# A four-layer adaLN block on one core: where the inputs are turned, where the keys come from, and four reordered slots

## The chip, the core and the metric

The kernel runs on 1 core of a Trainium2 chip. A core has five engines, each with an instruction stream of its own that is worked off in order: TensorE (PE in the profile; PEld is its weight load), VectorE (DVE), ScalarE (ACT), GpSimd (POOL) and SyncE (SP), which here only issues DMAs. ACT and POOL issue DMAs too. Engines wait for one another by semaphores. The metric is the device time of one execution in microseconds (us). Before the change three timed runs gave 6840.84, 6856.30 and 6861.61 us, with the median 6856.3.

## What is computed

The reference is a stack of four layers on x of 32 sequences x 256 positions x 128 features, all in float32. Each layer has an attention half and a feed-forward half, each wrapped in adaptive layer norm:

```python
mod = (_silu(Ln_c) @ Ln_wmod).reshape(32, 6, 1, 128)      # shift, scale, gate, twice
sa, ca, ga, sb, cb, gb = (mod[:, i] for i in range(6))
g* = (2 * (g* >= 0) - 1) * jnp.maximum(jnp.abs(g*), 0.25)
x = x + ga * attn(_layernorm(x) * (1 + ca) + sa)
x = x + gb * ffn(_layernorm(x) * (1 + cb) + sb)
```

The change touches three places of it. The beginning reads x and makes the modulations of the four layers. Layer 0's attention half is a selective scan (h = exp(delta A) h + delta u B, y = C h, over 256 positions, 16 states for each feature, two branches that share the scan), with delta and u from a softplus. Layer 1's attention half has a windowed softmax attention and five sets of causal linear attention: the plain keys and values, and four levels of keys and values averaged over blocks of 2, 4, 8 and 16, each set with features phi(k) = elu(k) + 1, a running sum over the sequence in chunks of 128, and a division by the norm. The other halves (two mixtures of experts, two more attentions, a grouped MLP, an fp4 MLP) are not touched.

## The kernel before

x is cut into 16 tiles of 512 positions (two sequences), and kept turned (features on the partitions) in on-chip memory for the whole run; `self.mods` keeps all modulations. `run` calls `begin`, then one body per half.

`begin` loads the c and wmod of all four layers in one DMA on ACT's queue, makes the four layers' modulations (six matmuls each, then copies on ACT and six operations on DVE for each of two halves), and turns the 16 tiles: one load each, by turns on SP's and ACT's queue with three buffers, four transposes on PE, and a copy by turns on DVE and ACT. Its pools close before those of the next body open.

`scan_layer` and `hale` are each an agenda: work is put under a slot number, and slots are emitted in order. PE's instructions keep exactly this order (`mm` and `tr` ask for it), in the scan ACT's too. Instructions of DVE and POOL and DMAs do not: a scheduler (the tile framework's) places them in their engine's stream by its own estimate of when they are ready, so a slot number alone does not tell where they stand.

In `scan_layer`, tile b's scan occupies slots 16b to 16b+15, and its preparation (two layer norms, projections, softplus for u and delta, B and C spread) slots 16b-40 to 16b; so 40 slots lead in before the first scan. A pass p (two slots, 8 passes a tile) is: 16 matmuls into `dB`, four DVE scans from `dB` and four `decay` tiles that ACT made a pass earlier, and, for the pass before, two sets of eight transposes into `hT` (one buffer), two ACT copies to `hsT`, and two sets of matmuls (`scan_weigh`) that add into `y`. `dB`, `hT`, `y` and `tp` have one PSUM buffer each. The softplus is split: `soft_start` makes |v+b| on ACT and max(v+b, 0) on DVE from a PSUM tile `tp`, `soft_end` makes ln(1+exp(-|v+b|)) on ACT and adds on POOL. A tile ends with `scan_end` in slot 16b+19: four transposes, an addition on DVE, two operations on POOL, and the residual on DVE.

In `hale`, a half-tile q (one sequence, T = 16q) runs through slots T-27 to T+28. The matmuls of scores and of weighted values are the `main` and `last` lists; projections, level keys and values, states and divisions are the `side` list that is fitted between. What matters here: `hale_values`, `hale_level_values` and `hale_level_keys` project values and keys; `kt` holds the keys with positions on the partitions, `a["f"]` the features of q, k and the four level keys with heads on the partitions; `hale_states` multiplies `kt` with the values of the first 128 positions and keeps the block diagonal in `kvs`. A head has 16 columns in `kvs`, of which 8 hold values, one holds the norm and 7 are never read as results. The mixture of experts before it leaves its outputs in memory; `gather_rows` fetches them for a tile with eight indirect DMAs that POOL issues, into `got` (one buffer), `gather_sum` weighs and adds them on DVE into `gy` (one buffer), and `gather_end` turns them and adds them to x.

Of the kernel before, what the change touches and what calls it, by code (L numbers as in the profile page):

```python
# [25 lines left out]
ALU = mybir.AluOpType  # L26
# [149 lines left out]
def packs(d):  # L176
# [8 lines left out]
    k.add("cT", np.stack([np.asarray(d[f"L{n}_c"]).T for n in range(4)], 1))  # L185
    k.add("wmod", np.stack([np.asarray(d[f"L{n}_wmod"]) for n in range(4)], 1))
# [33 lines left out]
    k.add("vvk", np.concatenate([g["Wv"].T, g["Wvl"].T, by_heads(g["Wk"].T, DENSE)], 1))  # L220
# [89 lines left out]
class Program:  # L310
# [291 lines left out]
    def begin(self):  # L602
        nc, tc = self.nc, self.tc
        nc.scalar.preload_act_table_set(LN_EXP)
        with ExitStack() as ctx:
            self.pools(ctx, {"tp": 4, "mod": 2}, xin=3, mw=1)
            mw = self.wk("mw", (P, self.at["mod"]["n"]))
            nc.scalar.dma_start(mw, self.aps["mod"])
            v = View(mw, self.at["mod"]["at"])
            for n in range(4):  # L610
                sg = self.wk("sg", (P, NSEQ))
                self.sigmoid(sg, v.cT[:, n, :])
                nc.vector.tensor_tensor(sg, sg, v.cT[:, n, :], ALU.mult)
                ps = self.ps("mod", (P, 6, NSEQ))
                for j in range(6):
                    nc.tensor.matmul(ps[:, j, :], v.wmod[:, n, j * P : (j + 1) * P], sg, start=True, stop=True)
                m = self.mods[:, n]
                for j in (0, 3):
                    nc.scalar.copy(m[:, j, :], ps[:, j, :])
                    nc.vector.tensor_scalar(m[:, j + 1, :], ps[:, j + 1, :], 1.0, None, ALU.add)  # L620
                    neg, mag = self.wk("neg", (P, NSEQ)), self.wk("mag", (P, NSEQ))
                    nc.vector.tensor_scalar(neg, ps[:, j + 2, :], -1.0, None, ALU.mult)
                    nc.vector.tensor_tensor(mag, ps[:, j + 2, :], neg, ALU.max)
                    nc.vector.tensor_scalar(mag, mag, 0.25, 2.0, ALU.max, ALU.mult)
                    nc.vector.tensor_scalar(neg, ps[:, j + 2, :], 0.0, 0.5, ALU.is_ge, ALU.subtract)
                    nc.vector.tensor_tensor(m[:, j + 2, :], neg, mag, ALU.mult)
            xd = self.aps["x"].rearrange("(b t p) f -> b p t f", p=P, t=4)
            for b in range(NB):
                xi = self.wk("xin", (P, 4, P))
                (nc.sync if b % 2 else nc.scalar).dma_start(xi, xd[b])  # L630
                ps = self.ps("tp", (P, 4, P))
                for t in range(4):
                    nc.tensor.transpose(ps[:, t, :], xi[:, t, :], self.c.ident)
                (nc.scalar.copy if b % 2 else nc.vector.tensor_copy)(self.x[b], ps.rearrange("p a b -> p (a b)"))


    def scan_layer(self, w):
# [7 lines left out]
        with ExitStack() as ctx:  # L645
            self.pools(
                ctx, {"dB": 1, "hT": 1, "y": 1, "tp": 1},
                h=4, z=3, dl=3, duT=3, bc=3, xn=1, ln_xn=1, xp=1, y=1, yT=1, rows=1, Xc=1, du=1, sg=1, hsT0=1, hsT1=1, sp_m=1, sp_r=1, Xr=1,
# [85 lines left out]
    def soft_start(self, src, bias):  # L734

        m, r = self.wk("sp_m"), self.wk("sp_r")
        self.act(m, src, AF.Abs, bias=bias)
        self.nc.vector.tensor_scalar(r, src, bias, 0.0, ALU.add, ALU.max)
# [89 lines left out]
    def scan_even(self, s, p):  # L828
# [70 lines left out]
    def scan_end(self, s, a):  # L899
# [4 lines left out]
        y = self.wk("y")  # L904
# [9 lines left out]
        self.residual(0, 0, a["b"], y)  # L914
# [319 lines left out]
    def gather_rows(self, b):  # L1234

        got = self.wk("got", (P, 4, 2, P))
        for t in range(4):
# [9 lines left out]
        self.gather[b] = got  # L1247
# [296 lines left out]
    def hale(self, w):  # L1544
        nc, c = self.nc, self.c
        BF = mybir.dt.bfloat16
        with ExitStack() as ctx:
# [18 lines left out]
            self.kvs = wk("kvs", (P, 5, SEQ))  # L1566
            self.kt = wk("kt", (P, 5, P))
# [21 lines left out]
    def hale_slots(self, w):  # L1589
# [9 lines left out]
        for q in range(2 * NB):  # L1599
# [207 lines left out]
    def hale_values(self, w, a, t):  # L1807

        n = 3 if t == 0 else 2
        pv = self.ps("tp", (P, n, P))  # L1810
        self.mm(pv, a["h"][:, t * P : (t + 1) * P], w.vvk[:, 0 : n * P])
        self.nc.vector.tensor_copy(
            self.vzb[t][:, :, :, 0:8], pv[:, 0:2, :].rearrange("p n (h d) -> p n h d", d=8)
        )
        if t == 0:
            self.phi(self.kt[:, 0, :], pv[:, 2, :])

    def hale_level_values(self, a, t, pair):

        if t == 0:  # L1820
            pv = self.ps("tp", (P, 2, 2, P))
            for l in (0, 1):
                lvl = 2 * pair + l
                self.mm(pv[:, l], a["hm"][:, lvl, 0:P], self.wl[:, lvl])
            lv = slice(2 * pair, 2 * pair + 2)
            src = pv[:, :, 1, :]
            self.phi(self.kt[:, 1 + 2 * pair : 3 + 2 * pair, :], pv[:, :, 0, :])
        else:
            src = self.ps("tp", (P, 4, P))
            for lvl in range(4):  # L1830
                self.mm(src[:, lvl, :], a["hm"][:, lvl, P:], self.wl[:, lvl, 1, :])
            lv = slice(0, 4)
        self.nc.vector.tensor_copy(self.vzl[t][:, lv, :, 0:8], src.rearrange("p l (h d) -> p l h d", d=8))
# [27 lines left out]
    def hale_states(self, a, ns):  # L1861

        pk = self.ps("tp", (P, len(ns), SEQ))
        for m, n in enumerate(ns):
            self.mm(pk[:, m, :], self.kt[:, n, :], self.set_values(n, 0)[:, :, 0:16])
        self.nc.vector.tensor_tensor(
            self.kvs[:, ns[0] : ns[-1] + 1, :],
            pk,
            self.c.same.unsqueeze(1).to_broadcast([P, len(ns), SEQ]),
# [931 lines left out]
```

## Time and profile before

| what | us |
|---|---|
| three timed runs, median | 6856.3 |
| the profiled execution, its own time | 6756.19 |
| its span, first to last instruction | 6754.3 |
| `begin` (0 to 45.5) | 45.5 |
| lead-in of the scan (45.5 to the first DVE scan at 125.0) | 79.5 |
| scans of 16 tiles (125 to 1158) | 1033 |
| mixture of experts (1158 to 1714) | 556 |
| `hale`, start (1714 to 1770) and slots (1770 to 3800) | 56 and 2030 |

Busy time over three of these stretches, with the granted TensorE clock (1.00 is full speed):

| stretch | PE | DVE | ACT | POOL | clock |
|---|---|---|---|---|---|
| 45.5 to 125 | 39.15 of 79.5 | 11.99 | 39.02 | 32.51 | 0.50 |
| 125 to 1158 | 785.31 of 1033 | 705.72 | 822.76 | 539.18 | 0.96 |
| 1770 to 3800 | 1938.98 of 2030 | 1261.91 | 959.34 | 898.07 | 0.98 |

A row of the profile's list of groups names line, engine and operation, output<-input with shapes, the count, busy time and mean duration, and then the idle time of the engine before these instructions with what ended it. A row of the timeline has start, duration, engine, line, operation and count, and in brackets how long the engine had been idle and what released it. A float32 matmul shows as two instructions.

### The profile page before, as it was taken

Reading aid. Unit: us, or ns where it says so; the run is one execution under the profiler, and the core shown is the slowest. Engines: PE = TensorE matmul, PEld = TensorE weight load, DVE = VectorE, ACT = ScalarE, POOL = GpSimd, SP = SyncE. Lnnn points to the kernel's source line nnn. Section 1 sums busy time; section 2 is a strip of 40 time slices with the busy share of each in tenths; the row PEclk is TensorE's granted clock in tenths of the full one; section 3 lists DMA queues with packets and bytes.
Section 4 is the critical chain, followed back from the end, with each engine's and each line's share of the span. In section 5 each row is a group of like instructions: output and inputs, shape, how many; then the busy total and the mean of one; then the engine's idle time right before and its main releaser. Section 6 shows DMA issues by size and latency. Waiting matters only on the chain. (4 is left out here: it accounts for less than half of the span.)

```text
span 6754.3 us, 132930 instructions
## 1 busy us (share of the span) xinstructions
PE 5907.4 (87%) x54209; PEld 3313.6 (49%) x54209; DVE 4350.0 (64%) x10025; ACT 3557.5 (53%) x5227; POOL 2660.5 (39%) x2881
## 2 busy tenths in 40 slices
PE   5777776899899999999999887999889998999987
PEld 3555555457555555555566444454422222444444
DVE  3666766621466666666666572888677774777779
ACT  5888885233344444444445442444478886544532
POOL 3555553566444444444444362444244543000000
PEclk7999998899899999999999877999999998989988
DMA  1101101135100000000000101111133442000010
GB/s 60 41 28 41 41 29 36 41 109 134 28 7 5 5 5 8 5 5 8 5 2 2 45 4 38 25 27 28 31 84 90 92 91 48 15 18 18 18 33 30
DMA packets 175447, 232.27 MB, mean 34 GB/s; under 512 B 46519, under 2 KB 95919, under 8 KB 174450
## 3 DMA queue, kind: packets, MB, share of 16 engines
q1 hardware_dynamic: 120656, 124.47, 7.3%
q0 software_dynamic: 26992, 56.62, 3.6%
q10 hardware_dynamic: 27186, 42.67, 1.7%
q8 instruction: 426, 6.98, 0.4%
q14 instruction: 187, 1.53, 0.1%
HBM read 88.28 MB, written 74.97 MB: 24 GB/s over the span
## 5 line engine op out<-in xcount | busy, mean ns | idle before, releaser
L1416 ACT ACTIVATE E<-S 128x1024 f32<-128x1024 f32 x448 | 459.0, 1025 | 592.8 <-PE S L386 579.4
L847 DVE TENSOR_TENSOR_SCAN hs<-decay,dB 128x512 f32<-128x512 f32 x512 | 583.1, 1203 | 196.9 <-PE dB L386 114.7
L298 DVE TENSOR_REDUCE mt<-S 128x4 f32<-128x1024 f32 (+1 forms) x512 | 550.2, 1088 | 224.5 <-PE S L386 223.8
L386 PE MATMUL S<-qa,kx 32*128 32x256 f32 x4096 | 556.2, 392 | 59.6 <-DVE mt L298 59.1
L393 ACT ACTIVATE hid<-S,bigw 128x1024 f32<-128x1024 f32 x512 | 537.6, 1112 | 124.2 <-PE S L386 124.0
L1888 DVE TENSOR_TENSOR E<-S,cst 128x1024 f32<-128x1024 f32 x320 | 391.2, 1223 | 301.1 <-PE S L386 300.5
L1891 POOL TENSOR_SCALAR_AFFINE_SELECT E<-E 128x1024 f32<-128x1024 f32 x320 | 350.2, 1094 | 594.6 <-ACT E L1890 594.2
L386 PE MATMUL S<-kx,q 32*128 32x512 f32 (+1 forms) x2048 | 540.4, 623 | 17.1 <-ACT kx L1534 16.1
L1890 ACT COPY E<-S 128x1024 f32<-128x1024 f32 x320 | 323.7, 1012 | 315.1 <-PE S L386 315.1
L2440 POOL TENSOR_TENSOR acc<-acc,ye 128x512 f32<-128x512 f32 x256 | 344.7, 1347 | 360.4 <-DVE ye L298 318.1
L386 PEld LDWEIGHTS S<-qa,kx 32*128 32x128 f32 x4096 | 350.8, 195 | 174.6 <-DVE mt L298 137.1
L1713 DVE TENSOR_REDUCE mt<-S 128x4 f32<-128x512 f32 (+1 forms) x256 | 205.2, 823 | 294.0 <-PE S L386 293.8
L386 PE MATMUL S<-qG,f 32*128 32x512 f32 x2560 | 382.3, 657 | 7.5 <-DVE E L1888 6.4
L386 PE MATMUL S<-hm,bigw 32*128 32x512 f32 x2048 | 338.7, 654 | 25.2 <-ACT hid L393 25.2
L393 ACT ACTIVATE hsT<-hT 128x1024 f32<-128x1024 f32 x256 | 260.4, 1017 | 179.7 <-PE hT L390 179.4
L390 PE MATMUL hT<-cst,hs 128*128 128x128 f32 x2048 | 285.9, 283 | 75.4 <-ACT hsT L393 73.5
L393 ACT ACTIVATE decay<-dl,A 128x510 f32<-128x510 f32 x512 | 339.2, 714 | 0.0
L386 PE MATMUL po<-E,vzl 128*32 128x128 f32 x8192 | 284.1, 279 | 50.1 <-POOL E L1891 50.1
L1760 ACT ACTIVATE E<-S 128x768 f32<-128x768 f32 (+1 forms) x192 | 169.1, 881 | 280.7 <-PE S L386 279.9
L390 PEld LDWEIGHTS hT<-cst,hs 128*128 128x128 f32 x2048 | 225.1, 143 | 169.6 <-ACT hsT L393 139.7
L386 PE MATMUL po<-E,vz 128*32 128x256 f32 x4096 | 300.2, 379 | 7.2 <-POOL E L1420 6.9
L386 PE MATMUL po<-hid,bigw 128*32 128x512 f32 x2048 | 277.2, 613 | 30.4 <-DVE ye L298 30.4
(520 smaller groups left out, 13307.8 us busy)
## 6 DMA issues: line engine op xcount, KB each, us to landing
gb<-gT SPq DMA_DIRECT2D x256, 256.0 KB
regions<-zeros ACTq DMA_DIRECT2D x16, 2048.0 KB
rx<-far SPq DMA_DIRECT2D x64, 256.0 KB
expert_rows<-eo SPq DMA_DIRECT2D x39, 256.0 KB
out<-out SPq DMA_DIRECT2D x16, 256.0 KB
xTd<-xT SPq DMA_DIRECT2D x15, 256.0 KB
xT<-xTd SPq DMA_DIRECT2D x15, 256.0 KB
bigw<-in_s SPq DMA_DIRECT2D x10, 256.0 KB
```

The source lines that it names most:

```text
L298: return lambda *args, **kw: self.tc.keep_in_program_order(op(*args, **kw))
L386: return self.tc.keep_in_program_order(self.nc.tensor.matmul(out, lhsT, rhs, start=start, stop=stop, **kw))
L390: return self.tc.keep_in_program_order(self.nc.tensor.transpose(out, in_, self.c.ident[:k, :k]))
L393: ins = self.nc.scalar.activation(*args, **kw)
L847: nc.vector.tensor_tensor_scan(hs[:, :, n], decay, dB[:, :, n], 0.0, ALU.mult, ALU.add)
L1416: nc.scalar.activation(e, src, AF.Exp, scale=scale)
L1713: nc.vector.tensor_reduce(m.rearrange("p (g j) -> p g j", j=2), pm[:, :, x] if i == 0 else pm[:, :, :, 0:192], AX.X, ALU.max, negate=True,)
L1760: nc.scalar.activation(e, src, AF.Exp, scale=1.0 / math.sqrt(8))
L1888: nc.vector.tensor_tensor(e, src, self.c.caus.unsqueeze(1).to_broadcast([P, 8, P]), ALU.mult)
L1890: nc.scalar.copy(e, src)
L1891: nc.gpsimd.affine_select(e, e, [[0, 8], [1, P]], ALU.is_ge, 0.0, base=0, channel_multiplier=-1)
L2440: nc.gpsimd.tensor_tensor(a["acc"], a["acc"], ye, ALU.add)
```

## The change

- `begin` makes the modulations of layer 0 and turns tile 0 only. The other 15 tiles are loaded in slots 2b-47 and turned in 2b-45 of the scan's agenda, through the PSUM buffer `dB`, all copied by DVE and all loaded on SP's queue with two buffers. Layers 1 to 3 are loaded in slots 8n-52 (ACT's queue, one buffer) and made in 8n-46, through the PSUM buffer `y`.
- `soft_start` no longer has an ACT operation: DVE makes r = max(v+b, 0) and then v - 2r, from which exp(v - 2r + b) is the same as before.
- In `scan_even` the matmuls of `scan_weigh` stand behind the transposes and the decay. The residual of the scan is put into slot 16b+21.
- In `hale` the gather of a tile is put as four quarters from T-62 on, the sums from T-52 on.
- The position-major keys `kt` are no longer projected and passed through phi: the features are turned (`hale_turn_keys`). All level values come from 128-column matmuls. `hale_states` makes 9 of the 16 columns of each head, and `kvs` is cleared once.

```diff
     def begin(self):
-        nc, tc = self.nc, self.tc
-        nc.scalar.preload_act_table_set(LN_EXP)
+        self.nc.scalar.preload_act_table_set(LN_EXP)
+        some = 0 in self.stages
         with ExitStack() as ctx:
-            self.pools(ctx, {"tp": 4, "mod": 2}, xin=3, mw=1)
-            mw = self.wk("mw", (P, self.at["mod"]["n"]))
-            nc.scalar.dma_start(mw, self.aps["mod"])
...
-            for b in range(NB):
-                xi = self.wk("xin", (P, 4, P))
-                (nc.sync if b % 2 else nc.scalar).dma_start(xi, xd[b])
-                ps = self.ps("tp", (P, 4, P))
-                for t in range(4):
-                    nc.tensor.transpose(ps[:, t, :], xi[:, t, :], self.c.ident)
-                (nc.scalar.copy if b % 2 else nc.vector.tensor_copy)(self.x[b], ps.rearrange("p a b -> p (a b)"))
+            self.pools(ctx, {"tp": 4, "mod": 2}, xin=3, mw=2)
+            for n in (0,) if some else range(4):
+                self.mod_layer(n, self.mod_load(n), self.ps("mod", (P, 6, NSEQ)))
+            for b in (0,) if some else range(NB):
+                self.turn_in(b, self.load_in(b), self.ps("tp", (P, 4, P)))
+    def mod_load(self, n):
+        mw = self.wk("mw", (P, NSEQ + 6 * P))
+        self.nc.scalar.dma_start(mw, self.aps["mod"][:, n * (NSEQ + 6 * P) : (n + 1) * (NSEQ + 6 * P)])
+        return mw
...
+    def load_in(self, b):
+        xi = self.wk("xin", (P, 4, P))
+        self.nc.sync.dma_start(xi, self.aps["x"].rearrange("(b t p) f -> b p t f", p=P, t=4)[b])
+        return xi
+    def turn_in(self, b, xi, ps):
+        for t in range(4):
+            self.tr(ps[:, t, :], xi[:, t, :])
+        self.nc.vector.tensor_copy(self.x[b], ps.rearrange("p a b -> p (a b)"))
...
     def scan_layer(self, w):
+            for b in range(1, NB):
+                put(2 * b - 47, lambda b=b: s.update({("xi", b): self.load_in(b)}))
+                put(2 * b - 45, lambda b=b: self.turn_in(b, s["xi", b], self.ps("dB", (P, 4, P))))
+            for n in (1, 2, 3):
+                put(8 * n - 52, lambda n=n: s.update({("mw", n): self.mod_load(n)}))
+                put(8 * n - 46, lambda n=n: self.mod_layer(n, s["mw", n], self.ps("y", (P, 6, NSEQ))))
...
                 put(T + 19, self.scan_end, s, a)
+                put(T + 21, lambda a: self.residual(0, 0, a["b"], a["y"]), a)
...
     def soft_start(self, src, bias):
-        self.act(m, src, AF.Abs, bias=bias)
         self.nc.vector.tensor_scalar(r, src, bias, 0.0, ALU.add, ALU.max)
-        return m, r
-    def soft_end(self, out, m, r):
-        self.act(m, m, AF.Exp, scale=-1.0)
+        self.nc.vector.scalar_tensor_tensor(m, r, -2.0, src, ALU.mult, ALU.add)
+        return m, r, bias
+    def soft_end(self, out, m, r, bias):
+        self.act(m, m, AF.Exp, bias=bias)
...
     def scan_even(self, s, p):
-        self.scan_weigh(s, p - 2, 1)
         self.scan_turned(s, p - 1, 0)
         self.scan_decay(s, p + 1, 0)
+        self.scan_weigh(s, p - 2, 1)
...
     def scan_end(self, s, a):
-        self.residual(0, 0, a["b"], y)
...
             self.kvs = wk("kvs", (P, 5, SEQ))
+            nc.gpsimd.memset(self.kvs, 0.0)
...
-                    put(side, T - 48, lambda b=b: self.gather_rows(b))
-                    put(side, T - 38, lambda b=b: self.gather_add(0, b))
+                    for t in range(4):
+                        put(side, T - 62 + 4 * t, lambda b=b, t=t: self.gather_rows(b, (t,)))
+                        put(side, T - 52 + 4 * t, lambda b=b, t=t: self.gather_sum(b, (t,)))
+                    put(side, T - 38, lambda b=b: self.gather_end(0, b))
...
-            put(side, T - 3, lambda a=a: self.hale_level_values(a, 0, 0))
-            put(side, T - 2, lambda a=a: self.hale_level_keys(a, 0))
-            put(side, T - 2, lambda a=a: self.hale_states(a, (0, 1)))
-            put(side, T + 0, lambda a=a: self.hale_level_keys(a, 1))
-            put(side, T + 1, lambda a=a: self.hale_level_values(a, 0, 1))
-            put(side, T + 2, lambda a=a: self.hale_level_values(a, 1, None))
-            put(side, T + 3, lambda a=a: self.hale_states(a, (2, 3)))
-            put(side, T + 4, lambda a=a: self.hale_states(a, (4,)))
+            put(side, T - 3, lambda a=a: self.hale_level_keys(a, 0))
+            put(side, T - 2, lambda a=a: self.hale_level_keys(a, 1))
+            put(side, T + 0, lambda a=a: self.hale_level_values(a, 0))
+            put(side, T + 1, lambda a=a: self.hale_turn_keys(a, (0, 1, 2)))
+            put(side, T + 2, lambda a=a: self.hale_level_values(a, 1))
+            put(side, T + 3, lambda a=a: self.hale_turn_keys(a, (3, 4)))
+            put(side, T + 4, lambda a=a: self.hale_states(a, (0, 1, 2)))
+            put(side, T + 5, lambda a=a: self.hale_states(a, (3, 4)))
...
     def hale_values(self, w, a, t):
-        n = 3 if t == 0 else 2
-        pv = self.ps("tp", (P, n, P))
-        self.mm(pv, a["h"][:, t * P : (t + 1) * P], w.vvk[:, 0 : n * P])
+        pv = self.ps("tp", (P, 2, P))
+        self.mm(pv, a["h"][:, t * P : (t + 1) * P], w.vv)
...
-            self.phi(self.kt[:, 0, :], pv[:, 2, :])
-            self.phi(self.kt[:, 1 + 2 * pair : 3 + 2 * pair, :], pv[:, :, 0, :])
+    def hale_level_values(self, a, t):
+        pv = self.ps("tp", (P, 4, P))
+        for lvl in range(4):
+            self.mm(pv[:, lvl, :], a["hm"][:, lvl, t * P : (t + 1) * P], self.wl[:, lvl, 1, :])
+    def hale_turn_keys(self, a, ns):
+        pk = self.ps("tp", (P, len(ns), P))
+        for m, n in enumerate(ns):
+            self.tr(pk[:, m, :], a["f"][:, 1 + n, 0:P])
+        self.nc.scalar.copy(self.kt[:, ns[0] : ns[-1] + 1, :], pk)
...
     def hale_states(self, a, ns):
-        pk = self.ps("tp", (P, len(ns), SEQ))
+        pk = self.ps("tp", (P, len(ns), 16, 9))
-            self.mm(pk[:, m, :], self.kt[:, n, :], self.set_values(n, 0)[:, :, 0:16])
+            self.mm(pk[:, m], self.kt[:, n, :], self.set_values(n, 0)[:, :, 0:9])
```

The weight packs follow: c and wmod stand layer by layer in one array, and `vvk` (values, local values and keys) becomes `vv` without the keys.

More of the change, by code (lines that the diff above doesn't have):

```diff
@@ L184, in packs @@
     k = Pack()
-    k.add("cT", np.stack([np.asarray(d[f"L{n}_c"]).T for n in range(4)], 1))
-    k.add("wmod", np.stack([np.asarray(d[f"L{n}_wmod"]) for n in range(4)], 1))
+    k.add("mod", np.stack([np.concatenate([np.asarray(d[f"L{n}_c"]).T, np.asarray(d[f"L{n}_wmod"])], 1) for n in range(4)], 1))
     out["mod"] = k
@@ L219, in packs @@
     k.add("Wv", g["Wv"])
[L220 removed]
+    k.add("vv", np.concatenate([g["Wv"].T, g["Wvl"].T], 1))
     k.add("haar_Wk", np.stack([by_heads(diag_blocks(g["haar_Wk"][lvl].T, 16), DENSE) for lvl in range(4)], 1))
@@ L602, in begin @@
     def begin(self):
-        nc, tc = self.nc, self.tc
-        nc.scalar.preload_act_table_set(LN_EXP)
+        self.nc.scalar.preload_act_table_set(LN_EXP)
+        some = 0 in self.stages
         with ExitStack() as ctx:
-            self.pools(ctx, {"tp": 4, "mod": 2}, xin=3, mw=1)
-            mw = self.wk("mw", (P, self.at["mod"]["n"]))
-            nc.scalar.dma_start(mw, self.aps["mod"])
[L609 to L627, printed above, removed]
-            for b in range(NB):
-                xi = self.wk("xin", (P, 4, P))
-                (nc.sync if b % 2 else nc.scalar).dma_start(xi, xd[b])
-                ps = self.ps("tp", (P, 4, P))
-                for t in range(4):
-                    nc.tensor.transpose(ps[:, t, :], xi[:, t, :], self.c.ident)
-                (nc.scalar.copy if b % 2 else nc.vector.tensor_copy)(self.x[b], ps.rearrange("p a b -> p (a b)"))
@@ new lines, in mod_layer @@
+    def mod_layer(self, n, mw, ps):
+        nc = self.nc
+        sg = self.wk("msg", (P, NSEQ))
+        self.sigmoid(sg, mw[:, :NSEQ])
+        nc.vector.tensor_tensor(sg, sg, mw[:, :NSEQ], ALU.mult)
+        for j in range(6):
+            self.mm(ps[:, j, :], mw[:, NSEQ + j * P : NSEQ + (j + 1) * P], sg)
+        m = self.mods[:, n]
+        for j in (0, 3):
+            nc.scalar.copy(m[:, j, :], ps[:, j, :])
+            nc.vector.tensor_scalar(m[:, j + 1, :], ps[:, j + 1, :], 1.0, None, ALU.add)
+            neg, mag = self.wk("neg", (P, NSEQ)), self.wk("mag", (P, NSEQ))
+            nc.vector.tensor_scalar(neg, ps[:, j + 2, :], -1.0, None, ALU.mult)
+            nc.vector.tensor_tensor(mag, ps[:, j + 2, :], neg, ALU.max)
+            nc.vector.tensor_scalar(mag, mag, 0.25, 2.0, ALU.max, ALU.mult)
+            nc.vector.tensor_scalar(neg, ps[:, j + 2, :], 0.0, 0.5, ALU.is_ge, ALU.subtract)
+            nc.vector.tensor_tensor(m[:, j + 2, :], neg, mag, ALU.mult)
@@ L647, in scan_layer @@
                 ctx, {"dB": 1, "hT": 1, "y": 1, "tp": 1},
-                h=4, z=3, dl=3, duT=3, bc=3, xn=1, ln_xn=1, xp=1, y=1, yT=1, rows=1, Xc=1, du=1, sg=1, hsT0=1, hsT1=1, sp_m=1, sp_r=1, Xr=1,
+                h=4, z=3, dl=3, duT=3, bc=3, xn=1, ln_xn=1, xp=1, y=1, yT=1, rows=1, Xc=1, du=1, sg=1, hsT0=1, hsT1=1, sp_m=1, sp_r=1, Xr=1, mw=1,
             )
@@ L903, in scan_end @@
             self.tr(py[:, i, :], a["yT"][:, i, :])
-        y = self.wk("y")
+        y = a["y"] = self.wk("y")
         cut = dict(i=4, r=32)
@@ L1232, in block_out, with gather_rows @@
             self.nc.sync.dma_start(m["eo"][j * n : (j + 1) * n, :].rearrange("(t p) f -> p t f", p=P), eo)
-    def gather_rows(self, b):
-        got = self.wk("got", (P, 4, 2, P))
-        for t in range(4):
+    def gather_rows(self, b, quarters=range(4)):
+        if 0 in quarters:
+            self.gather[b] = self.wk("got", (P, 4, 2, P))
+        got = self.gather[b]
+        for t in quarters:
             for k in (0, 1):
@@ L1246, in gather_rows @@
                 )
-        self.gather[b] = got
     def gather_add(self, layer, b):
@@ L1807, in hale_values @@
     def hale_values(self, w, a, t):
-        n = 3 if t == 0 else 2
-        pv = self.ps("tp", (P, n, P))
-        self.mm(pv, a["h"][:, t * P : (t + 1) * P], w.vvk[:, 0 : n * P])
[L1812 to L1815, printed above, removed]
-            self.phi(self.kt[:, 0, :], pv[:, 2, :])
[L1818 to L1826, printed above, removed]
-            self.phi(self.kt[:, 1 + 2 * pair : 3 + 2 * pair, :], pv[:, :, 0, :])
[L1828 to L1833, printed above, removed]
+        pv = self.ps("tp", (P, 2, P))
+        self.mm(pv, a["h"][:, t * P : (t + 1) * P], w.vv)
+        self.nc.vector.tensor_copy(self.vzb[t][:, :, :, 0:8], pv.rearrange("p n (h d) -> p n h d", d=8))
+    def hale_level_values(self, a, t):
+        pv = self.ps("tp", (P, 4, P))
+        for lvl in range(4):
+            self.mm(pv[:, lvl, :], a["hm"][:, lvl, t * P : (t + 1) * P], self.wl[:, lvl, 1, :])
+        self.nc.vector.tensor_copy(self.vzl[t][:, :, :, 0:8], pv.rearrange("p l (h d) -> p l h d", d=8))
+    def hale_turn_keys(self, a, ns):
[3 more added lines that the diff above has]
+        self.nc.scalar.copy(self.kt[:, ns[0] : ns[-1] + 1, :], pk)
     def hale_features(self, w, a):
@@ L1861, in hale_states @@
     def hale_states(self, a, ns):
-        pk = self.ps("tp", (P, len(ns), SEQ))
+        pk = self.ps("tp", (P, len(ns), 16, 9))
         for m, n in enumerate(ns):
-            self.mm(pk[:, m, :], self.kt[:, n, :], self.set_values(n, 0)[:, :, 0:16])
+            self.mm(pk[:, m], self.kt[:, n, :], self.set_values(n, 0)[:, :, 0:9])
+        same = self.c.same.rearrange("p (h d) -> p h d", d=16)[:, :, 0:9]
         self.nc.vector.tensor_tensor(
-            self.kvs[:, ns[0] : ns[-1] + 1, :],
+            self.kvs[:, ns[0] : ns[-1] + 1, :].rearrange("p n (h d) -> p n h d", d=16)[:, :, :, 0:9],
             pk,
-            self.c.same.unsqueeze(1).to_broadcast([P, len(ns), SEQ]),
+            same.unsqueeze(1).to_broadcast([P, len(ns), 16, 9]),
             ALU.mult,
```

## The prediction

> **What bounds the kernel.** I read the busy time by stretches first, then the groups, then the engines' timelines inside one scan tile and one half-tile of `hale`. The changed and the old program's instruction orders tell what really moves.
>
> ```profile
> 45.50:125.00 79.50, 39.15 (x117) 16.77 (x118) 11.99 (x49) 39.02 (x83) 32.51 (x57) 0.50 0.01 2
> 125.00:1158.00 1033.00, 785.31 (x11058) 548.95 (x11057) 705.72 (x861) 822.76 (x1346) 539.18 (x635) 0.96 0.10 37
> 1770.00:3800.00 2030.00, 1938.98 (x21724) 1184.90 (x21723) 1261.91 (x2423) 959.34 (x1594) 898.07 (x956) 0.98 0.02 5
> ```
>
> Columns: stretch, its length, busy PE, PEld, DVE, ACT, POOL, the clock, DMA share, GB/s. Three regimes. In the lead-in no engine is half busy and PE runs at half clock: a chain of latencies sets it. In the scans ACT is busiest (80%), DVE has 68%, and nobody is full: a loop of waits. In `hale` PE has 95.5%: what PE no longer issues is gained there, if nothing else turns up. The rest (MoE, and all behind 3800) has the same instructions; I cost it at 0.
>
> **Begin and lead-in.**
>
> ```profile
> 13.48 2.58 PE L633 MATMUL tp<-cst,xin 128*128 128x128 f32 x11 [13.48 <-DMA xin<-in_x]
> ...
> 43.91 1.09 PE L633 MATMUL tp<-cst,xin 128*128 128x128 f32 x4 [2.31 <-DMA xin<-in_x]
> ...
> 46.82 1.11 PE L390 MATMUL tp<-cst,x 128*128 128x128 f32 x4 [0.36 <-ACT wd L658]
> ```
>
> The first norm (46.82) stands behind 16 loads on two queues. Afterwards it needs one layer's c and wmod (0.41 MB of 1.6), the constants, a first part of w and one tile (0.26 MB): 2 MB, by 8 us (5 to 10 us ran at 407 GB/s), then mods and turn; the norm's statistics on DVE stand behind two more turned tiles and layer 1's sigmoid, whose load ACT issues at about 10: some 17.5. Gain 29. From there to `u`'s projection took 34.3 us (46.8 to 81.1), and that chain now carries 15 turns (four cold transposes 1.09, DVE copy about 0.7 behind them, one `dB`) and three layers (12 cold matmul passes 2.6 each, ACT copies queued ahead of the norms' waiting for them). Added one behind the other that is 15 x 1.8 + 3 x 4.2 = 40; in the orders most lie in gaps of a stretch in which PE idles 40 of 79.5; my walk through it puts 11 us on the path. Ends: 0 and 21. The loads must keep up too: two buffers, issue to landing 2.8 to 4.9 us, so about 2.7 us a tile or 38 us for the last 14, which fits; SP has no other transfer before the scans' own, and the three loads that ACT issues take an engine that is busy 39 of 79.5. Net **-18** (-8 to -28).
>
> **Scan, per tile (64.8 us).**
>
> ```profile
> 516.26 0.75 DVE L738 TENSOR_SCALAR sp_r<-tp,w 128x512 f32<-128x512 f32 x1 [1.42 <-ACT sp_m L393]
> 516.93 4.55 DVE L847 TENSOR_TENSOR_SCAN hs<-decay,dB 128x512 f32<-128x512 f32 x4
> 522.29 0.69 DVE L906 TENSOR_TENSOR y<-uu,tp 128x512 f32<-128x512 f32 x1 [0.80 <-PE tp L390]
> 527.69 1.53 DVE L533 SCALAR_TENSOR_TENSOR x<-y,mods,x 128x256 f32<-128x256 f32 x2 [4.71 <-POOL y L913]
> 529.14 4.54 DVE L847 TENSOR_TENSOR_SCAN hs<-decay,dB 128x512 f32<-128x512 f32 x4
> ```
>
> DVE waits 4.71 us for POOL once a tile, with the next scans queued behind the residual. *The residual's move* to slot 16b+21 should end that, but the scheduler places DVE's instructions: in the built program the residual stands where it stood in all 16 tiles, directly behind `y<-uu,tp` and ahead of the scans. I cost it at 0. *Softplus:* four Abs (0.57 to 0.67 on ACT) go, four DVE operations come. No row of before has that operation. Below: 0.69 (`y<-uu,tp`, a PSUM and an SBUF input, same size) to 0.75 (`sp_r`). Above: 1.38, as `sg<-xp,sg` took beside POOL against 0.73 alone. The Trainium skill (GPSIMD Engine Reference, the table of the engine's numbers) says the SBUF interfaces shared with VectorE contend when a DVE instruction has two SBUF inputs; `sg<-xp,sg` has two, the new one has one, so I take the low end, 0.7 (by the other 4 x 0.7 x 16 = 45 more on DVE, a part of it on the path). It stands ahead of a set of scans and `tp` is free 0.7 later. Walked over the tile's eight scan sets (they start 6.6 to 12.2 us apart): sets that wait for PE or DVE come 0.7, 0.6, 0.3, 0.1 later, the 4.71 wait swallows the rest. *Weighing behind the turns:* `hT` is asked for earlier by some 16 matmuls, -0.25, -0.15, and where ACT is full (489.6 to 502.9) one Abs less is -0.57 there. Sum about -0.3 a tile, **-5** for 16; ends -16 and +13 (the walk's parts are each as large as its sum).
>
> **Hale, per half-tile.** PE is in order, so its rows can be exchanged one by one:
>
> ```profile
> 2106.98 1.13 PE L386 MATMUL tp<-wl,hm 128*128 128x256 f32 x4
> ...
> 2110.63 0.66 PE L390 MATMUL tp<-cst,oc 128*128 128x128 f32 x4
> 2111.13 1.06 PE L386 MATMUL tp<-wl,hm 128*128 128x128 f32 x8
> ...
> 2114.70 1.13 PE L386 MATMUL tp<-vzl,kt 128*128 128x256 f32 x4
> 2115.67 0.38 PE L390 MATMUL tp<-cst,mt 128*128 128x128 f32 x2
> ```
>
> Start to start a row costs a little less than its duration (a shorter slot's 1.06 or 0.97 below). Two level pairs of 256 columns (1.06 each) become one set of four levels by 128 (1.11 by the x8 row): -1.01. Five states of 256 columns (0.86, 0.97, 0.53 by their slots) become five of 144, 0.27 each by columns: -1.03. The keys' 128 of 384 columns in `hale_values`: 0.85 to 0.63, -0.22. Five turns come, 0.67 (0.50 for the four above): **-1.6**, x32 = -51. ACT's phi for `kt` becomes one copy; DVE's multiplications by the mask shrink (681 ns for 512 columns); so the other engines get lighter and the waits are short: in a half-tile without gather PE is busy 60.78 of 61.75.
>
> Here a rule speaks against the change. The Trainium skill (TensorE: Matmul & The Clock Gate, Part 4: PE-mode transpose) has a 128x128 transpose at about 275 ns in a kernel and says that the mode doesn't count as busy for the clock gate. By it five cost 1.38, the sum is -1.6 + 0.7 = -0.9, or -29, with a clock that may sink. The rows say 0.50 for four pipelined ones (though each has some 280 ns as its duration), and 1.00 of granted clock over 2076 to 2138, where turns of `oc` and `mt` run all along. I take the rows; -29 goes into the range.
>
> **The gather.** Quarters from T-62 on should spread POOL's eight indirect DMAs, whose pile stalls PE once a tile:
>
> ```profile
> 2015.03 1.03 POOL L1239 DMA_INDIRECT got<-expert_rows,back  x1 [3.30 <-DVE gy L1262]
> ...
> 2022.04 1.00 POOL L1239 DMA_INDIRECT got<-expert_rows,back  x1 [0.30 <-issue]
> 2023.05 1.10 POOL L1891 TENSOR_SCALAR_AFFINE_SELECT E<-E 128x1024 f32<-128x1024 f32 x1
> 2024.32 1.00 POOL L1239 DMA_INDIRECT got<-expert_rows,back  x1 [0.16 <-issue]
> ```
>
> ```profile
> 2024.21 0.64 PE L386 MATMUL po<-E,vzl 128*32 128x128 f32 x16 [4.17 <-POOL E L1891]
> ```
>
> The select of `E` sits behind six DMAs on POOL and PE's `po` behind the select: 4.17. Half-tiles with the pile take 68.25, without 61.75. But `got` and `gy` have one buffer: the first DMA is released by DVE's `gy` (3.30) however early its slot is, and in the built program all quarters follow one another, now *seven* DMAs ahead of the select and one behind, in 12 tiles. So the pile stays and the wait grows by one DMA, 1.3 us (1.00 and 0.30): **+14** to +16. The clearing of `kvs` (1 us on POOL, ahead of the first gathers) is +1. Hale: -51 + 15 = -36.
>
> **Sum.** -18 - 5 - 36 = -59 against the profiled execution (6756.19), so 6697 for a profiled one. The timed runs lie 100 us (1.5%) above it; scaled, -60: 6856.3 - 60 = **6796**, I write 6795.
>
> **The rivals.**
> *Hale gives its PE time back* (0.20). Fewer PE instructions between `S` and `po` bring PE sooner to `E`, which ACT and POOL make; a DVE reduction and two-buffer pools could set the pace. For: PE waits 4.2 for `E` at the pile. Against: elsewhere only 0.3 to 0.6 a half-tile, and DVE has 62% of the stretch, ACT 47%. If two thirds of the 51 go: -60 + 34 = -26, about 6832 (6818 to 6846).
> *Slower* (0.08): the clock. If transposes and shorter passes make the gate read PE as idle in `hale`, each 0.01 of 2010 us is 20 us; from 0.03 on the whole gain is gone, at 0.05 it is +40: 6896. For: the half-tile with the stall has 0.97, that without 1.00, so the gate does answer to what PE does there. Against: 1.00 with two dozen turns in it.
> *The slots hold* (0.06): residual and gather stand where they are put on the chip's clock after all: the stall of 4.77 x 16 = 76 and 6.5 x 12 = 78 with the 14 not paid go as well: 6795 - 168, about 6627. Against: the two orders.
>
> **How the numbers follow.** My own case has 0.66: 6795, of itself 6765 to 6825 (lead-in +-10, scan +-13, keys +22). The range takes in the rival with lost PE time and the lower half of what a partly shorter stall would bring: 6745 to 6846. No change means within 0.3% (20 us, about what this measurement can tell). All of my case and half of the first rival and the last are faster: 0.66 + 0.10 + 0.06 = 0.82; same 0.10; slower 0.08.
>
> **What would show it.** First DVE scan near 107 instead of 125. A scan tile within 0.8 us of 64.8, with DVE's wait for POOL `y` still 4 to 5 us and about 0.7 for the new operation. Half-tiles of `hale` without pile near 60.2, with it near 68; the wait for POOL `E` at the pile about 5.5; clock at 0.98. If tiles lack the pile, or the 4.71 wait, I have misread what the orders mean; if half-tiles keep 61.75 with PE less busy, the first rival holds; if the clock row falls to 0.95, the slower one.

## The result, and the profile after

Seven timed runs of the changed kernel have the median 6810.6 us (6797.61 to 6831.59), seven of the kernel before 6857.47 us; the ratio is 0.994 (0.9923 to 0.9957), taken from the means. That is faster by 47 us between the medians (29 to 53 by the ratio's interval), where 60 were forecast; 6795 was predicted with 6745 to 6846 as the range.

The profiled execution of the changed kernel, however, has a span of 6808.6 us, 54 us more than the profile of before (6754.3). One execution against one would call the change slower. So the stages are compared first. They are cut at instructions that both kernels have (first and last DVE scan, first gather of the first mixture of experts, first and last reading of `kvs`, first and last gather of the second):

| stage | before | before, profiled again | after |
|---|---|---|---|
| to the first scan | 125.0 | 121.0 | 110.2 |
| first to last scan | 1018.1 | 1017.2 | 1010.0 |
| to the first gather | 585.6 | 599.1 | 603.9 |
| to the first reading of `kvs` | 83.1 | 83.5 | 81.2 |
| `hale`, first to last reading of `kvs` | 2011.8 | 2006.6 | 1977.4 |
| second mixture, to its first gather | 335.2 | 369.6 | 371.8 |
| layer 2's attention, to its last gather | 546.5 | 603.1 | 599.9 |
| the rest | 2049.0 | 2047.9 | 2054.2 |

The three stages in which after is much longer (the first mixture, the second one and layer 2's attention) have the same instructions in both kernels. The middle column (the first experiment) shows that they are as long without the change, to within 5 us: it is the first profile of before that was taken under better conditions. The rest is 5 to 6 us longer in after; it took between 2040 and 2060 in the other profiles, so that is within what single profiles scatter. The touched stages got shorter by 14.8, 8.1, 1.9 and 34.4 us against the first profile, 59 in all, and by 10.8, 7.2, 2.3 and 29.2, some 50, against the second.

The stretches of the profile after, with busy PE, PEld, DVE, ACT and POOL, the clock, DMA share and GB/s as before:

```profile
110.20:1134.00 1023.80, 806.80 (x11058) 570.12 (x11057) 734.93 (x918) 800.78 (x1287) 538.82 (x635) 0.92 0.11 38
...
1763.00:3763.00 2000.00, 1895.51 (x21934) 1173.24 (x21932) 1182.83 (x2269) 933.20 (x1473) 895.58 (x957) 0.98 0.02 5
```

ACT is busy 22 us less in the scans (the Abs), DVE 29 more, and PE 43 us less in `hale`, in a window that is 30 us shorter. The clock in `hale` is 0.98 as before.

**The lead-in**, PE's timeline:

```profile
18.43 1.09 PE L389 MATMUL dB<-cst,xin 128*128 128x128 f32 x4 [3.94 <-DMA xin<-in_x]
20.30 1.12 PE L389 MATMUL dB<-cst,xin 128*128 128x128 f32 x4 [0.78 <-DVE x L646]
21.21 1.06 PE L389 MATMUL tp<-cst,x 128*128 128x128 f32 x4
...
65.61 2.07 PE L385 MATMUL tp<-u,wd 128*128 128x512 f32 x2 [0.79 <-POOL u L764]
```

Tile 0's first norm starts at 21.21 instead of 46.82. In PE's order the turns of tiles 1 and 2 (into `dB`) stand ahead of it, and tile 1's load lands only at 18.4. From there to `u`'s projection it takes 44.4 us, where it took 34.3. The first scan stands at 110.2.

**A scan tile**, DVE's timeline:

```profile
501.70 0.69 DVE L758 SCALAR_TENSOR_TENSOR sp_m<-sp_r,tp 128x512 f32<-128x512 f32 x1
...
507.09 0.69 DVE L926 TENSOR_TENSOR y<-uu,tp 128x512 f32<-128x512 f32 x1 [0.23 <-PE tp L389]
512.73 1.55 DVE L532 SCALAR_TENSOR_TENSOR x<-y,mods,x 128x256 f32<-128x256 f32 x2 [4.95 <-POOL y L933]
514.20 4.54 DVE L867 TENSOR_TENSOR_SCAN hs<-decay,dB 128x512 f32<-128x512 f32 x4
```

The new operation (`sp_m<-sp_r,tp`) takes 0.69. The residual, put two slots later, still stands ahead of the scans and waits 4.95 us for POOL.

**The gather in `hale`**, POOL's timeline, and PE's row that waits for it:

```profile
2003.43 1.04 POOL L1260 DMA_INDIRECT got<-expert_rows,back  x1 [2.91 <-DVE gy L1282]
...
2011.29 1.00 POOL L1260 DMA_INDIRECT got<-expert_rows,back  x1 [0.30 <-issue]
2012.31 1.10 POOL L1908 TENSOR_SCALAR_AFFINE_SELECT E<-E 128x1024 f32<-128x1024 f32 x1
2013.57 1.27 POOL L1260 DMA_INDIRECT got<-expert_rows,back  x1 [0.16 <-issue]
```

```profile
2013.46 1.08 PE L385 MATMUL po<-E,vzl 128*32 128x128 f32 x16 [4.94 <-POOL E L1908]
```

Seven DMAs, one every 1.3 us, then the select, then one DMA: the pile is there, one DMA taller, and PE waits 4.94 where it waited 4.17.

**The keys**, PE's timeline of a half-tile:

```profile
2094.63 0.55 PE L389 MATMUL tp<-cst,f 128*128 128x128 f32 x3
2095.11 0.53 PE L385 MATMUL po<-E,vzb 128*32 128x192 f32 x8
```

A transpose shows as one instruction. From start to start, these three turns of keys take 0.48 us; the other two, at 2101.76, take 0.28.

### The profile page after: what moved, and what is told of

Its sections match the earlier page's. It is cut to its first block, busy times and chain, and to the rows that moved or that the text cites. A ratio compares the mean times of both kernels' runs of the same rounds, so it can differ in the third digit from the quotient of the medians.

```text
span 6808.6 us, 132864 instructions
## 1 busy us (share of the span) xinstructions
PE 5935.8 (87%) x54369; PEld 3351.9 (49%) x54369; DVE 4297.3 (63%) x9937; ACT 3496.0 (51%) x5026; POOL 2658.6 (39%) x2882
## 5 line engine op out<-in xcount | busy, mean ns | idle before, releaser
L385 PE MATMUL S<-qa,kx 32*128 32x256 f32 x4096 | 570.2, 399 | 60.9 <-DVE mt L297 40.4
L389 PE MATMUL hT<-cst,hs 128*128 128x128 f32 x2048 | 303.8, 296 | 40.7 <-ACT hsT L392 39.7
L385 PE MATMUL po<-E,vzl 128*32 128x128 f32 x8192 | 286.5, 280 | 60.2 <-POOL E L1908 59.9
L1440 POOL TENSOR_SCALAR_AFFINE_SELECT E<-E 128x512 f32<-128x512 f32 (+1 forms) x192 | 158.3, 825 | 366.8 <-ACT E L1436 366.4
L389 PEld LDWEIGHTS hT<-cst,hs 128*128 128x128 f32 x2048 | 242.8, 150 | 113.7 <-ACT hsT L392 92.0
```

The costliest lines, as they stand in the source:

```text
L385: return self.tc.keep_in_program_order(self.nc.tensor.matmul(out, lhsT, rhs, start=start, stop=stop, **kw))
L389: return self.tc.keep_in_program_order(self.nc.tensor.transpose(out, in_, self.c.ident[:k, :k]))
L1440: nc.gpsimd.affine_select(part, part, [[0, n], [1, P]], ALU.is_ge, 0.0, base=0, channel_multiplier=-1)
```

## Experiments

Each was set beside runs of the kernel before on the same chip. The theory: the parts work as in the forecast's sum, and what differs between the two profiles beyond it is not the change's.

### Before again, and three parts alone

*Before, profiled once more.*

> The kernel before, unchanged, profiled a second time. Between the two profiles on hand, stages whose instructions the change leaves alone grew by 113 us (first MoE 19, layer 1's MoE 37, layer 2's attention 53). Theory A, those stages vary from execution to execution with the granted clock: this profile shows a span near 6855, with last PE read of kvs at 3820 to 3860, first gather of the second MoE's rows some 370 us later and the last some 600 after that (as in the profile of after). Theory B, the change slows them: the span is near 6754 again, with 335 and 547 us for those two stages.

6849.79 us, span 6848.0. Theory A holds: 369.6 us for the second mixture and 603.1 for layer 2's attention, as in the profile of after. The two windows of 400 us in layer 2's attention, the first profile of before and then this one, differ in the clock, and PE is busy in both:

```profile
4300.00:4700.00 400.00, 369.49 (x3565) 197.47 (x3564) 340.00 (x909) 182.56 (x235) 179.35 (x226) 0.95 0.14 28
```

```profile
4300.00:4700.00 400.00, 374.53 (x3298) 203.05 (x3290) 304.01 (x834) 166.71 (x216) 163.55 (x206) 0.88 0.12 25
```

PE's busy time is nearly the same, but it gets through 3298 instructions instead of 3565, at a clock of 0.88 instead of 0.95. Nothing in this stretch was edited.

*The beginning alone* (in the diff: `begin` and its new functions, the loads and turns in the scan's agenda).

> Before with only the new beginning (one tile, one layer, the rest in the lead-in). My step gave -18 in the lead-in, the profile of after has its first DVE scan at 110.2 instead of 125.0, so -15; theory A expects 6843 (ratio 0.998), first scan at 110. Rival: a part of what is gained is paid back by the scans, because the layers' and tiles' copies hold DVE and ACT up: then the ratio is 1.000 although the first scan stands at 110.

6841.39 us, ratio 0.9979 (0.9970 to 0.9988): -14 us. First scan at 107.4; first to last scan 1018.8 (1018.1 and 1017.2 in the two profiles of before), so nothing is paid back there.

*The keys alone* (`hale_turn_keys`, `hale_level_values`, the narrow `hale_states`, the clearing of `kvs`).

> Before with only hale's turned keys, 128-column level values and narrow states. My step gave -1.6 us a half-tile, -51 in all, by the rows; by the price of 275 ns a transpose it would be -29. The gather stays as before (pile of six DMAs). Theory A expects 6806 (ratio 0.9926), hale's clock still 0.98. Rival (PE's time given back to waits for S and E): ratio 0.996 or more, half-tiles without pile over 61.

6821.97 us, ratio 0.9943 (0.9924 to 0.9962); from first gather to the last reading of `kvs` 2062.1 us, 28 less than in before again; the timed ratio, with its interval, says 26 to 52 less. The clock is 0.98. The half-tiles tell why the stage is not 51 shorter. In a tile the gather falls into the first of its two half-tiles. From one projection of `dT` to the next, the second half-tile, without gather, went from 61.06 to 59.56 us, -1.50; the first, with gather, lay between 69.1 and 70.0 and now lies between 68.4 and 70.0, on average 69.35 and 69.34. (The forecast's 61.75 and 68.25 cut the half-tiles elsewhere; a whole tile is about 130 us either way.) PE's waits show the reason; the first row is before again, the second the keys alone (both 1820 to 3780; us in total, times, longest):

```profile
PE po L386 <- POOL E L1891: 44.6, 12, 3.8
```

```profile
PE po L386 <- POOL E L1885: 60.2, 12, 5.1
```

and POOL's timeline in the keys alone, where the gather's code is untouched:

```profile
2038.40 1.00 POOL L1239 DMA_INDIRECT got<-expert_rows,back  x1 [0.30 <-issue]
2039.41 1.11 POOL L1885 TENSOR_SCALAR_AFFINE_SELECT E<-E 128x1024 f32<-128x1024 f32 x1
2040.68 1.27 POOL L1239 DMA_INDIRECT got<-expert_rows,back  x1 [0.16 <-issue]
```

The DMA that starts at 2038.40 is the seventh; in before, and with the beginning alone, six stand ahead of the select and two behind it in all 12 of these tiles. So it is the keys edit that puts one more DMA ahead of the select. Which part of that edit makes the scheduler place it so (the other slots, the copies on ACT or the clearing on POOL) was not taken apart.

*Softplus and weighing.*

> Before with only the softplus without Abs and the weighing behind the turns; residual as before. My step gave -0.3 us a tile, -5 in all (-16 to +13); the profile of after has -8 between first and last scan. Theory A: ratio 0.999, DVE's wait for POOL y still 70 to 75 us, the new DVE operation 0.69. Rival (two edits that offset each other to nothing): ratio 1.000 and scans of 1018 us as before.

6848.57 us, ratio 0.9994 (0.9982 to 1.0006): not to be told from nothing by the time; first to last scan 1014.0, 3 us less. With the keys alone, where nothing of the scans is edited, this stretch took 1022.8, so a single profile doesn't settle 3 us.

### Gather and residual: undone, and made to happen

*The quarters undone:* after with `gather_rows(b)` in slot T-48 and `gather_add` in T-38 as before.

> After with the gather put back to one lump of eight in slot T-48 and one lump of sums. My forecast charged the seventh DMA ahead of the select (+14 us) to the quarters. The profile of the keys alone, where the gather is untouched, shows seven as well. Theory C (it is the keys edit that moves the select, the quarters do nothing): 6810, ratio 0.994, PE's wait for POOL E again 12 times near 5 us. My forecast's reading: six DMAs, wait 45 to 50 us instead of 60, time 6796.

6814.34 us, ratio 0.9943 (0.9929 to 0.9956), the same as after; the same seven DMAs, select and one DMA in 12 tiles, and PE waits 60.8 us for POOL's `E` (59.9 in after). The quarters do nothing.

*The quarters truly spread:* each gather DMA and each select is held behind the operation ahead of it in the slots.

```diff
-                self.nc.gpsimd.indirect_dma_start(
+                self.pool_order(self.nc.gpsimd.indirect_dma_start(
...
+    def pool_order(self, ins):
+        if self.spread:
+            before = [i for i in self.nc.cur_bb.bb.instructions if i is not ins.ins
+                      and i.engine == ins.ins.engine and "RegisterMove" not in type(i).__name__]
+            self.tc.add_manual_dep(ins.ins, before[-1].name, ...
```

> After, with the gather's DMAs and the selects of E held on POOL in the order of their slots (quarters truly spread, two DMAs at a time; nothing else changed). If the pile is what costs 5 us a tile, PE's waits for POOL E (60 us) go, hale gets 50 to 60 us shorter, the ratio is 0.986. Rival: the DMAs' waits for the sums now stop POOL at other selects, or PE meets the next wait (ACT oc, DVE E): a gain below 20 us, 0.992.

6840.46 us, ratio 0.998 (0.9972 to 0.9988): 30 us *slower* than after. PE's and then DVE's waits (1850 to 3340):

```profile
PE S L385 <- DVE E L1922: 62.5, 34, 4.2
```

```profile
DVE gy L1296 <- DMA got<-expert_rows,back: 78.3, 33, 4.7
```

The wait for POOL's `E` (59.9 in after) is gone from the list; a wait of the same size for DVE's `E` stands in its place. DVE's sums of each quarter are now placed close behind their DMAs, and their two operations wait 78 and 22 us for landings, with DVE's `E` queued behind them. The rival had named DVE's `E` as the next wait, but with a gain left over; neither theory had DVE's waits for landings, and after's list has none among its largest. The half-tiles show where the time went: the first of a tile falls to 61.89 us, as in the tiles without a gather, and the second rises from 59.56 to between 67.5 and 74.

*The residual truly behind the scans:* DVE's scans and the residual keep the order of their slots.

```diff
-                nc.vector.tensor_tensor_scan(hs[:, :, n], decay, dB[:, :, n], ...)
+                self.tc.keep_in_program_order(nc.vector.tensor_tensor_scan(hs[:, :, n], decay, dB[:, :, n], ...))
...
+    def scan_resid(self, a):
+        self.nc.vector.on = True
+        self.residual(0, 0, a["b"], a["y"])
+        self.nc.vector.on = False
```

> After, with DVE's scans and the residual held in the order of their slots, so that the residual stands behind one set of scans instead of ahead of it. The wait for POOL y (16 times 4.7, 75 us) should fall to under 1 us each. Theory D, the wait is on the path: scans 1010 to about 940, ratio 0.985. Rival: PE's dB and ACT's decays set the scans' rhythm and the wait is a gap that they fill: dB waits grow by as much and the ratio stays at 0.993.

6743.77 us, ratio 0.9834 (0.9818 to 0.9849): 67 us faster than after. First to last scan 942.6 instead of 1010.0. DVE's timeline:

```profile
486.58 0.69 DVE L931 TENSOR_TENSOR y<-uu,tp 128x512 f32<-128x512 f32 x1 [0.24 <-PE tp L389]
487.79 4.56 DVE L867 TENSOR_TENSOR_SCAN hs<-decay,dB 128x512 f32<-128x512 f32 x4 [0.52 <-PE dB L385]
492.35 1.54 DVE L297 SCALAR_TENSOR_TENSOR x<-y,mods,x 128x256 f32<-128x256 f32 x2
```

DVE's waits for `dB` (130 to 1100), in after and then here:

```profile
DVE hs L867 <- PE dB L385: 177.9, 86, 5.0
```

```profile
DVE hs L867 <- PE dB L385: 179.9, 100, 4.7
```

Theory D holds: POOL's two operations lie beside the next scans, and the residual finds `y` ready (its waits for POOL fall from 72.0 us to 2.8). The rival had the waits for `dB` grow by as much; they grow by 2 us.

*Both.*

> Both of the other two edits on after. They lie in different stages, so the gains add: 0.978 if theories of the pile and of the residual hold, 0.985 if one of them does, 0.992 if neither.

6768.27 us, ratio 0.9876 (0.9860 to 0.9891): the residual's gain and the spread's loss add.

### Sums later, and turns twice

These two ran on a chip on which the kernel before took 6758.59 us (nine runs), near its first profile; ratios are to that, and layer 2's attention took 556 us in both.

*Sums later:* both edits, and on DVE the first operation of each quarter's sum is held behind what stands before it in the slots.

```diff
+            was, nc.vector.on = nc.vector.on, nc.vector.on or self.spread
             nc.vector.tensor_scalar(y[:, t, :], got[:, t, 0, :], self.pair[:, 0, at], None, ALU.mult)
+            nc.vector.on = was
```

> The run with spread gather and moved residual, and the first operation of each quarter's sum on DVE held behind what stands before it in the slots, so that it doesn't wait for its DMA's landing. In the spread run DVE waited 116 us for landings and PE 73 us for DVE's E instead of 60 for POOL's. Theory: with the sums ten slots behind their DMAs both waits go; hale 1925 to 1935 instead of 1980, 6690, ratio 0.976. Rival: the sums or the turning of gy stop another chain, hale over 1970, ratio 0.983.

6561.68 us, ratio 0.970 (0.9685 to 0.9715), the fastest of all: 1.8 times the distance from before that the residual alone has. `hale` takes 1905.4, 72 us less than in after and more than expected. PE's waits (1850 to 3340):

```profile
PE S L385 <- DVE E L1929: 21.4, 38, 1.2
```

No wait for POOL's `E` and no wait of DVE for a landing is left among the largest; the first half-tile of a tile takes 61.89 instead of 68.4 to 70, as it does in a tile without a gather, and the second 60.67 instead of 59.56: over the 12 tiles with a pile that is 76 us less. The clock of this stretch is 1.00, against 0.98. That is no second gain beside the stall's. Where no gather is left, near the end, after and this run take the same (61.89 and 59.56), and the next run, on the same chip and with the pile, has first half-tiles of 69.6 to 69.9 and a clock of 0.97 in this window.

*Turns twice:* each key transpose is issued twice into the same place.

```diff
-        for m, n in enumerate(ns):
-            self.tr(pk[:, m, :], a["f"][:, 1 + n, 0:P])
+        for _ in (0, 1):
+            for m, n in enumerate(ns):
+                self.tr(pk[:, m, :], a["f"][:, 1 + n, 0:P])
```

> After with each of the five key transposes of a half-tile issued twice into the same place (160 transposes more, the result unchanged). By the row (0.13 us each, pipelined) 21 us more than after: ratio 0.997; by the page's 275 ns 44 us more: ratio 1.000; if transposes cost the clock gate, the clock of hale falls below 0.97 and more is lost.

6725.98 us, ratio 0.995 (0.9935 to 0.9965); a ratio of 0.994 without the doubling came from another chip, so the half-tile decides. The second half-tile of a tile went from 59.56 to 60.10: 0.54 for five transposes, 0.11 each. (The first, in the two tiles without gather where it can be compared, went from 61.89 to 62.10.) PE's timeline:

```profile
2083.42 0.87 PE L389 MATMUL tp<-cst,f 128*128 128x128 f32 x6
2084.23 0.53 PE L385 MATMUL po<-E,vzb 128*32 128x192 f32 x8
```

Six take 0.81 from start to start, where three took 0.48; four take 0.49. The clock from 1900 to 3600 us is 0.98 in after and here. A cost of 0.275 us each, or a sinking clock, is refuted for transposes that stand between other matmuls, as these do.

### Softplus and weighing apart

> Before with the softplus alone (Abs gone from ACT, one operation more on DVE). The pair of edits took the scans from 1017 to 1014. By my walk the softplus alone is close to nothing (later sets 0.7, 0.6, 0.3, 0.1 a tile, ACT's 0.57 back, the wait for y swallowing the rest): scans 1015 to 1021. Rival: ACT was the bound and the whole gain is the softplus's: scans 1013 or less.

6867.15 us, ratio 1.0006 (0.9993 to 1.0018); scans 1017.7. It does nothing, though four operations of 0.68 us a tile left the busiest engine (its exponential, now with a bias, takes 0.71 instead of 0.63). DVE's waits (130 to 1100), before again and then the softplus alone:

```profile
DVE hs L847 <- PE dB L386: 109.9, 73, 2.3
DVE hs L847 <- ACT decay L393: 67.2, 19, 4.3
```

```profile
DVE hs L847 <- PE dB L386: 170.6, 85, 3.7
...
DVE hs L847 <- ACT decay L393: 11.3, 5, 3.6
```

The scans' wait for ACT's decays fell by 56 us, and that for `dB` rose by 61: what ACT gave back went to the next thing that a scan waits for. ACT itself waits 177 us for PE's `hT` in this window instead of 160. Why `dB` is later (DVE holds `tp` for one operation more, which was argued in the forecast) was not tried by itself.

> Before with the weighing behind the turns and the decay alone. By my walk -0.4 us a tile: scans 1011. Rival: nothing by itself, scans 1016 to 1018.

6848.53 us, ratio 0.9983 (0.9974 to 0.9992), scans 1009.0: 8 us less. What the scans gain comes from the weighing: with the residual where it was, the stretch takes 1017 to 1023 in the profiles without it and 1009 to 1014 in those with it.

## Why the prediction was right, step by step

- **The direction and the place of the gain** were right: lead-in, scans and `hale` each gained, and the rest is untouched. By parts, timed: -14 for the beginning; by stages -3 for softplus and weighing together (-7 in after) and -28 for the keys. They make 45 to 49 of the 47 measured; 60 was forecast. That the sum meets so well is partly luck: the three timed ratios alone give -58, with about 16 of noise.
- **Lead-in: the gain at tile 0's start was put too high.** -18 forecast, -14 timed; the first scan comes 15 us earlier than in the first profile of before, 11 than in the second, and 14 with the beginning alone. The chain of 45 us from norm to projection (34.3 and 11) was right (44.4). But the norm was put at 17.5, and starts at 21.21: PE's own order has the turns of two more tiles ahead of it, and the wait of 3.94 for tile 1's load, which the step had counted for DVE alone. So the gain there was 25.6 and not 29.
- **Scan: right, as far as single profiles tell.** -5 forecast, -7 measured; the residual at 0 (74.7 us of waiting for POOL `y` against 70.6); the new operation 0.69 in all 64 cases, by the row of one PSUM and one SBUF input, though POOL works beside about half of them; softplus alone nothing, weighing alone -8 where -6 was in the walk. That both together gave only -3 is within the scatter of some 5 us.
- **Hale: the row was right, the rule was not.** -1.6 a half-tile forecast, -1.50 measured in the second half-tiles. The transpose costs 0.11 to 0.16 us where it stands between other matmuls; the 275 ns of the Trainium skill (TensorE: Matmul & The Clock Gate, Part 4: PE-mode transpose) appear as each one's duration (273 to 301 ns on average, by group, in after), not as its cost. The page's measurement names bf16; here the data are float32. The rival of the sinking clock is out: the clock stays at 0.98 with the turns, and with twice as many.
- **The gather: right size, wrong edit.** "The wait grows by one DMA" was measured as 16 us over 12 tiles (44.6 to 60.2). But the step blamed the quarters. Undone, they change nothing; the keys alone bring the seventh DMA. The forecast compared two whole programs and charged what differed to the edit whose name fitted. Its sum was not hurt by that, because both edits are in the change. With the keys' -48 (32 times -1.5) and the pile's +16 the sum of `hale` is -32; the stages give -31 to -36.
- **The rival "hale gives its PE time back" holds in part.** Of the -48, a third went into the wait at the pile, by this one DMA. A general shortage hardly shows: PE's other waits in the same windows add up to 34 us in before again and 39 with the keys alone (ACT `oc` 18.7 and 18.5, DVE `E` 13.0 and 10.4; new are DVE `mt` with 6.6 and ACT `mT` with 3.5). -48, 16 and 5 make the -28 of that run to about a microsecond. (The rival's own sum gives 6830, where 6832 was written.)
- **The rival "the slots hold"** was rightly put low: both stalls are in after. Its price was nearly right: making them hold brought 67 us for the residual (76 forecast) and 72 in `hale` (92: 78 and the 14 not paid), but the second needed an edit that it had not named, the sums'. Without it the spread gather lost 30 us.

What stays open: which part of the keys edit moves the select behind the seventh DMA, why `dB` comes later with the softplus alone, and why the first scan of after stands 3 us later than with the beginning alone (109 to 111 in all runs made from after).

## What to carry to other kernels

Where a scheduler places an engine's instructions, a slot number is only a wish: a moved operation has moved only when it stands elsewhere in that engine's stream, and the profile's wait in front of it tells. Price a removed operation by what waits next (here `dB` for the decays, DVE's `E` for POOL's), and when a transfer is brought forward, look where its consumer is placed: too close behind the transfer, it stalls its engine as the pile did here (100 us of DVE's waiting for landings). Charge a difference between two programs to an edit only after that edit alone has shown it.

## What the hardware showed beyond that

The kernel before takes 6854 to 6861 us on three chips and 6759 on a fourth; its first profile, whose chip is not on record, has 6756. Between that profile and the second the difference lies in three stages: the two mixtures (13 and 34 us) and layer 2's attention (57). In windows of 400 us in layer 2's attention the granted clock is 0.87 to 0.89 in the slower profiles and 0.93 to 0.95 in the first profile and on the fourth chip, with PE busy 91 to 94% in all. Why the clock differs is not shown. Two such profiles can differ by twice what a change is worth; cut into stages at shared instructions they still tell it to some 5 us.

And a DVE operation with two SBUF inputs, `sg<-xp,sg`, took 1331 ns on average in the scans before and 844 after, though it is the same. What moved is its place beside POOL: in most tiles the first of two multiplications `Cd<-cst,bc` lies beside it for 0.83 us before and for 0.30 after, and in the last tile, with no work of POOL beside it, it takes 0.69 and 0.68.
